# Last cross-attention of a decoder: values moved ahead of the fourth score, the last half in two units of 256 queries, the next maxima begun inside a unit

## The chip, the cores and the metric

The kernel runs on one core of a Trainium2 chip. The metric is device time in microseconds (us) for one execution, the median of several. Engines are named as the profile names them: PE is TensorE (PEld its weight loads), DVE is VectorE, ACT is ScalarE, POOL is GpSimd, and SP issues most of the DMAs. [...]

## The reference

The reference is a decoder of four layers over 1024 tokens of width 128. Each layer has self-attention, cross-attention to a context of 6404 rows, and a feed-forward part, each with a layer norm before it and added to `x`. The change touches the cross-attention of the last layer, which has 16 heads of 8 columns:

```python
q = _split_heads(Q @ Wq.T + bq)          # 1024 queries
k = _split_heads(K @ Wk.T + bk)          # 6404 keys
v = _split_heads(V @ Wv.T + bv)
scores = jnp.einsum('bhqd,bhkd->bhqk', q, k) / np.sqrt(D_HEAD)
scores = jnp.where(mask == 0, -1e9, scores)
attn = jax.nn.softmax(scores, axis=-1)
ctx = jnp.einsum('bhqk,bhkd->bhqd', attn, v)
return ctx.reshape(b, s, h * d) @ Wo.T + bo
```

The softmax needs the largest score of every query and head before the exponentials. The kernel therefore computes the scores twice: once with queries on the partitions, for the maxima, and once with keys on the partitions, for the exponentials and the values.

## The kernel before

Twelve stages follow each other, and the last cross-attention (`l3_xattn`, line 1650) is the last but one. Its operands are prepared earlier. Every number is split into three bf16 parts, so that one bf16 matmul over 64 partitions gives a product of nearly float precision for one head. `qPs[g]` and `kPs[g % 2]` hold queries and keys of group `g`: a group has four heads, as two pairs, and a pair is one tile of 128 partitions, one head in rows 0 to 63 and the other in rows 64 to 127. Keys of two groups fit in SBUF; `pairs_read` (line 1249) fetches those of groups 2 and 3 through SP's DMA queue once groups 0 and 1 are done.

The work is cut into eight **units**: four groups of heads by two halves of 512 queries. One unit is one call of `pairs_core` (line 1304). It walks over 51 key tiles (50 of 128 keys and one of 4). For each key tile it issues, for each of four heads, a score matmul (tile `s`, 128 keys by 512 queries) and an exponential on ScalarE (L1352, into `p`). After the fourth head's score it issues the four value matmuls of the *previous* key tile (`values`), which add onto `acc`: four heads in four column groups of the PE, 9 columns each, the ninth giving the sum of the softmax.

Beside each unit run the **maxima of the next one** (`pairs_max`, line 1258): a generator of 52 steps, 13 chunks of 512 keys by four tiles of 128 queries. One step has two parts, one per pair; each part issues two matmuls into a tile `m2` and one reduction on VectorE (L1280). `pairs_core` takes one step per key tile, between the second head's score and the third. There being 52 steps and 51 key tiles, the last step comes after the last values. When the steps are used up, the generator runs `pairs_neg` (line 1285): it reduces the maxima (L1290), splits them into three bf16 parts with small VectorE operations (L1293 to L1296), transposes them on the PE (L1300), and adds them to rows of `qP` kept free for that (L1302), so that the next unit's score matmuls subtract the maxima by themselves. `pairs_norm` (line 1368) then transposes the unit's result, divides it by its sum, and writes it to `o`.

[...]`ps = _Psum(ps0, m2=2, s=3, acc=1)`. That is two tiles `m2` of two banks each, three tiles `s`, and one `acc`. A fourth score has to wait until the exponential that reads the oldest of the three `s` tiles is done.

The framework's scheduler orders the instructions of each engine by their place in the program, but takes a later one first where an earlier one is not ready. `self.matmul` (line 261) marks a matmul that must keep the program's order among those so marked on the PE; scores, maxima and values in this loop are all marked, the transposes are not.

The first layer's self-attention (`l0_attn`, line 519) uses the same functions with a causal mask, and the third layer's cross-attention uses `pairs_core` with exponentials of double width.

Of the kernel before, what the change touches and what calls it, by code (L numbers as in the profile page):

```python
# [10 lines left out]
F32 = mybir.dt.float32  # L11
BF16 = mybir.dt.bfloat16
# [7 lines left out]
P = 128  # L20
# [194 lines left out]
class Decoder:  # L215
# [303 lines left out]
    def l0_attn(self):  # L519
# [6 lines left out]
        with tc.tile_pool(name="a", bufs=2) as pool:  # L526
# [39 lines left out]
            with tc.tile_pool(name="a1", bufs=2) as pool1, tc.tile_pool(name="a1_ps", bufs=2, space=PSUM) as ps0:  # L566
                ps = _Psum(ps0, m2=2, s=3, acc=1)

                def maxima(n):
                    if n < 8:  # L570
                        return self.pairs_max(ps, pool1, qPs[n % 4], kPs[n % 4], n // 4, mpad, S, causal)
                    return ()

                for step in maxima(0):
                    step(0)
                    step(1)
                for n in range(8):
                    g, h = n % 4, n // 4
                    oT = pool1.tile([P, BANK], F32, tag="oT", name="oT")
                    self.pairs_core(ps, pool1, qPs[g], kPs[g], v, g, h, oT, AF.Exp, 64, maxima(n + 1), causal=causal)  # L580
                    self.pairs_norm(ps, pool1, oT, o, g, h)
            with tc.tile_pool(name="a2", bufs=2) as pool2, tc.tile_pool(name="a2_ps", bufs=2, space=PSUM) as ps0:
                self.small_out(_Psum(ps0, m=8), pool2, o, wo)

# [670 lines left out]
                at = 16 * (2 * g + i)  # L1255
                self.nc.sync.dma_start(out=t[:, a:b], in_=src[at:at + 16, :, a:b].rearrange("p i c -> (p i) c"))

    def pairs_max(self, ps, pool, qP, kP, h, mpad, nk=NK, causal=None):

        nc = self.nc
        chunks = h + 1 if causal is not None else (nk + BANK - 1) // BANK
        mx = pool.tile([P, 4, 4, chunks], F32, tag="mx", name="mx")
        for c in range(chunks):
            for t in range(4):
                q0 = h * BANK + t * P
                a, b = c * BANK, min((c + 1) * BANK, nk if causal is None else q0 + P)

                def step(pair, a=a, b=b, q0=q0, t=t, c=c):
                    diag = causal is not None and b == q0 + P
                    m = ps.tile([P, 2, BANK], F32, tag="m2", name="m2")
                    for j in range(2):
                        r = slice(64 * j, 64 * j + 64)
                        self.matmul(m[:, j, :b - a], lhsT=qP[pair][r, q0:q0 + P], rhs=kP[pair][r, a:b], start=True, stop=not diag)
                    if diag:
                        for j in range(2):
                            self.matmul(m[:, j, b - a - P:b - a], lhsT=causal[:, 1, :], rhs=causal[:, 0, :], start=False, stop=True)
                    nc.vector.tensor_reduce(mx[:, t, 2 * pair:2 * pair + 2, c:c + 1], m[:, :, :b - a], AX.X, ALU.max)  # L1280

                yield step
        self.pairs_neg(ps, pool, qP, h, mpad, mx)

    def pairs_neg(self, ps, pool, qP, h, mpad, mx):

        nc = self.nc
        r = pool.tile([P, 4, 4], F32, tag="r", name="r")
        part = pool.tile([P, 4, 4], BF16, tag="part", name="part")
        nc.vector.tensor_reduce(r, mx, AX.X, ALU.max, negate=True)  # L1290
        mp = mpad.rearrange("p a t (j r) -> p t a j r", r=64)
        for i in range(3):
            nc.vector.tensor_copy(part, r)  # L1293
            nc.vector.tensor_copy(mp[:, :, :, :, 7 + 8 * i], part.rearrange("p t (a j) -> p t a j", a=2))
            if i < 2:
                nc.vector.tensor_tensor(r, r, part, ALU.subtract)  # L1296
        m = ps.tile([P, 2, BANK], F32, tag="m2", name="m2")
        for pair in range(2):
            for t in range(4):
                nc.tensor.transpose(m[:, pair, t * P:(t + 1) * P], mpad[:, pair, t, :], self.ident)  # L1300
            q = qP[pair][:, h * BANK:(h + 1) * BANK]
            nc.vector.tensor_tensor(q, q, m[:, pair, :], ALU.add)  # L1302

    def pairs_core(self, ps, pool, qP, kP, v, g, h, oT, func, rows, beside=None, between=None, causal=None):

        nc = self.nc  # L1310
        acc = ps.tile([P, BANK], F32, tag="acc", name="acc")
        nc.vector.memset(acc, 0.0)
        wide = beside is None
        matmul = nc.tensor.matmul if wide else self.matmul
        beside = iter(beside or ())
# [4 lines left out]

        def values(t, n, off, ws):
            for j in range(4):
                matmul(acc[32 * j:32 * j + v.shape[3], off:], lhsT=v[:n, t, 4 * g + j, :], rhs=ws[j][:n, :BANK - off],  # L1323
                       start=t == 0, stop=t == nkt - 1, tile_position=(0, 32 * j))

        for t in range(nkt):
            n = min(P, nk - t * P)
            off = 0 if causal is None else max(t * P - h * BANK, 0)
            w, hs = BANK - off, slice(h * BANK + off, (h + 1) * BANK)
            diag = causal is not None and t >= 4 * h  # L1330
            step = next(beside, None)
            ws = []
            for pair in range(2):
                both = None
                if wide:
                    both = ps.tile([P, 2, BANK], F32, tag="s", name="s")
                    p2 = pool.tile([P, 2, BANK], F32, tag="p", name="p", bufs=5)
                    ss, pp = [both[:, 0, :], both[:, 1, :]], [p2[:, 0, :], p2[:, 1, :]]
                else:
                    ss = [ps.tile([P, BANK], F32, tag="s", name="s") for _ in range(2)]  # L1340
                    pp = [pool.tile([P, BANK], F32, tag="p", name="p", bufs=10) for _ in range(2)]
                for j in range(2):
                    r = slice(64 * j, 64 * j + rows)
                    matmul(ss[j][:n, :w], lhsT=kP[pair][r, t * P:t * P + n], rhs=qP[pair][r, hs], start=True, stop=not diag)  # L1344
                if diag:
                    for j in range(2):
                        matmul(ss[j][:, :P], lhsT=causal[:, 0, :], rhs=causal[:, 1, :], start=False, stop=True)
                if wide:
                    nc.scalar.activation(p2[:n], both[:n], func)  # L1349
                else:  # L1350
                    for j in range(2):
                        nc.scalar.activation(pp[j][:n, :w], ss[j][:n, :w], func)  # L1352
                ws += pp
                if step and pair == 0:
                    step(0)
                    step(1)
            if late:
                values(*late.pop(0))
            late.append((t, n, off, ws))
            if between is not None:  # L1360
                next(between, None)
        values(*late.pop(0))
        for step in beside:
            step(0)
            step(1)
        self.copy(oT, acc)

    def pairs_norm(self, ps, pool, oT, o, g, h):

        nc = self.nc  # L1370
        m = ps.tile([P, 2, BANK], F32, tag="m2", name="m2")[:, 0, :]
        for i in range(4):
            nc.tensor.transpose(m[:, i * P:(i + 1) * P], oT[:, i * P:(i + 1) * P], self.ident)
        mv = m.rearrange("p (t j r) -> p t j r", t=4, r=32)
        rd = pool.tile([P, 4, 4], F32, tag="rd", name="rd")
        nc.vector.reciprocal(rd, mv[:, :, :, 8])
        ov = o[:, 4 * h:4 * h + 4, 32 * g:32 * g + 32].rearrange("p t (j r) -> p t j r", r=8)
        nc.vector.tensor_tensor(ov, mv[:, :, :, 0:8], rd[:, :, :, None].to_broadcast([P, 4, 4, 8]), ALU.mult)

    def l2_xattn(self):  # L1380
        nc, tc = self.nc, self.tc
# [268 lines left out]
    def l3_xattn(self):  # L1650
# [5 lines left out]
        with tc.tile_pool(name="x", bufs=2) as pool:  # L1656
# [27 lines left out]
                    next(vs, None)  # L1684
            with tc.tile_pool(name="x1", bufs=2) as pool1, tc.tile_pool(name="x1_ps", bufs=2, space=PSUM) as ps0:
                ps = _Psum(ps0, m2=2, s=3, acc=1)

                def maxima(n):
                    if n < 8:
                        return self.pairs_max(ps, pool1, qPs[n // 2], kPs[n // 2 % 2], n % 2, mpad)  # L1690
                    return ()

                for n in range(8):
                    g, h = n // 2, n % 2
                    oT = pool1.tile([P, BANK], F32, tag="oT", name="oT")
                    self.pairs_core(ps, pool1, qPs[g], kPs[g % 2], v, g, h, oT, AF.Exp, 64, maxima(n + 1))
                    if h == 1 and g < 2:
                        self.pairs_read(kPs[g], kd, g + 2, NK)
                    self.pairs_norm(ps, pool1, oT, o, g, h)
            with tc.tile_pool(name="x2", bufs=2) as pool2, tc.tile_pool(name="x2_ps", bufs=2, space=PSUM) as ps0:  # L1700

                nc.vector.tensor_tensor(o, o, bv[:, None, :].to_broadcast([P, NT, D]), ALU.add)
# [94 lines left out]
```

## Time and profile before

| | |
|---|---|
| median of 3 runs | 6444.39 us (6440.16 to 6455.54) |
| profiled execution | 6445.11 us, span 6443.3 us, mean granted PE clock 0.942 |
| PE busy | 5978.2 us, 93% of the span |
| DVE busy | 3473.1 us, 54% |
| ACT busy | 2999.3 us, 47% |
| loop of the last cross-attention | from about 5229 us to 6250 us of the span |
| maxima reductions (L1280), whole kernel | 928 instructions, 1026.8 us |
| exponentials (L1352), whole kernel | 1824 instructions, 924.7 us |

The page's busy times cover the whole kernel, and most of them belong to stages that the change leaves alone. [...] The useful views are the chain of work that ended last, the timeline inside one unit, the groups of instructions with different shapes kept apart, and the table of stretches, which also gives the PE clock that was granted. In the timeline a row gives the start, the time from the first start to the last end of the instructions merged in it, the engine, line and shapes, and in brackets the idle time before and what ended it.

### The profile page before, as it was taken

Reading aid. Unit: us, or ns where it says so; the run is one execution under the profiler, and the core shown is the slowest. Engines: PE = TensorE matmul, PEld = TensorE weight load, DVE = VectorE, ACT = ScalarE, POOL = GpSimd, SP = SyncE. Lnnn points to the kernel's source line nnn. Section 1 sums busy time; section 2 is a strip of 40 time slices with the busy share of each in tenths; the row PEclk is TensorE's granted clock in tenths of the full one; section 3 lists DMA queues with packets and bytes.
Section 4 is the critical chain, followed back from the end, with each engine's and each line's share of the span. In section 5 each row is a group of like instructions: output and inputs, shape, how many; then the busy total and the mean of one; then the engine's idle time right before and its main releaser. Section 6 shows DMA issues by size and latency. Waiting matters only on the chain. (4 is left out here: it accounts for less than half of the span.)

```text
span 6443.3 us, 78699 instructions
## 1 busy us (share of the span) xinstructions
PE 5978.2 (93%) x30428; PEld 2195.2 (34%) x30428; DVE 3473.1 (54%) x6685; ACT 2999.3 (47%) x4049; POOL 2231.0 (35%) x1074
## 2 busy tenths in 40 slices
PE   6799999999999999999899968999988779999979
PEld 2233333434343434343475433111134211111126
DVE  5476666666666666664224152100024799999913
ACT  2323333343433333334211226999921048788872
POOL 1026766677776767678331530100001000000000
PEclk7699999999999999999989978999999779999999
DMA  3000000000000000000000013200002100000000
GB/s 101 4 1 1 1 1 1 1 1 1 1 1 1 1 1 1 1 6 7 32 5 10 1 61 93 69 16 1 1 7 77 52 1 21 1 21 1 1 6 28
DMA packets 60845, 102.46 MB, mean 16 GB/s; under 512 B 10014, under 2 KB 46134, under 8 KB 58422
## 3 DMA queue, kind: packets, MB, share of 16 engines
q1 hardware_dynamic: 59894, 94.16, 4.7%
q8 instruction: 238, 3.90, 0.3%
q10 hardware_dynamic: 576, 3.28, 0.2%
q14 instruction: 137, 1.12, 0.1%
HBM read 66.01 MB, written 31.34 MB: 15 GB/s over the span
## 5 line engine op out<-in xcount | busy, mean ns | idle before, releaser
L755 POOL TENSOR_TENSOR tot<-tot,p 128x1024 f32<-128x1024 f32 (+1 forms) x800 | 1886.1, 2358 | 669.2 <-ACT p L747 636.0
L674 DVE CUSTOM_DVE_ANT_0 junk<-m,bars 128x512 f32<-128x512 f32 (+1 forms) x1664 | 1112.8, 669 | 620.3 <-PE m L671 492.3
L747 ACT ACTIVATE p<-s,drop,keep 128x1024 f32<-128x1024 f32 (+1 forms) x416 | 501.1, 1205 | 1487.4 <-PE s L740 1473.8
L1280 DVE TENSOR_REDUCE mx<-m 128x2 f32<-128x1024 f32 (+4 forms) x928 | 1026.8, 1155 | 89.0 <-PE m L263 78.6
L1352 ACT ACTIVATE p<-s 128x512 f32<-128x512 f32 (+3 forms) x1824 | 924.7, 590 | 272.9 <-PE s L263 272.2
L671 PE MATMUL m<-kT,qT 64*128 64x512 f32 (+1 forms) x3328 | 942.0, 608 | 1.1 <-DVE mx L674 0.8
L735 PE MATMUL s<-qT,kT 64*128 64x512 f32 (+1 forms) x3264 | 832.9, 599 | 9.6 <-DVE p L745 9.6
L722 PE MATMUL acc<-p,v 128*64 128x512 f32 (+1 forms) x3264 | 791.2, 605 | 0.8 <-ACT p L747 0.8
L1349 ACT ACTIVATE p<-s 128x1024 f32<-128x1024 f32 (+1 forms) x816 | 751.1, 1172 | 23.9 <-PE s L1344 23.9
L745 DVE TENSOR_TENSOR p<-s,every 128x1024 f32<-128x1024 f32 x400 | 489.7, 1224 | 198.3 <-PE s L735 111.5
L1323 PE MATMUL acc<-p,v 128*8 128x512 f32 (+1 forms) x3264 | 552.1, 596 | 0.0
L747 ACT ACTIVATE p<-p,drop,keep 128x1024 f32<-128x1024 f32 x400 | 492.8, 1232 | 44.3 <-DVE p L745 44.1
L263 PE MATMUL m<-kP,qP 64*128 64x512 bf16 (+4 forms) x1856 | 372.7, 397 | 116.9 <-DVE mx L1280 57.1
L263 PE MATMUL acc<-p,v 128*9 128x512 f32 (+3 forms) x3648 | 476.6, 595 | 0.0
L671 PEld LDWEIGHTS m<-kT,qT 64*128 64x128 f32 x3328 | 306.2, 186 | 474.9 <-DVE mx L674 226.6
L735 PEld LDWEIGHTS s<-qT,kT 64*128 64x128 f32 (+1 forms) x3264 | 332.2, 187 | 396.1 <-issue 341.6
L263 PE MATMUL s<-qP,kP 64*128 64x512 bf16 (+3 forms) x1824 | 435.4, 387 | 31.6 <-ACT p L1352 28.8
L722 PEld LDWEIGHTS acc<-p,v 128*64 128x64 f32 (+1 forms) x3264 | 197.0, 136 | 530.3 <-issue 527.4
L269 DVE COPY oT<-acc 128x512 f32<-128x512 f32 x16 | 11.0, 688 | 536.9 <-PE acc L1323 301.3
L1344 PE MATMUL s<-qP,kP 48*128 48x512 bf16 (+1 forms) x1632 | 249.2, 383 | 1.6 <-ACT p L1349 1.6
L263 PEld LDWEIGHTS <-qP 64*128 64x128 bf16 x1856 | 122.7, 96 | 335.2 <-issue 265.9
L263 PEld LDWEIGHTS <-kP 64*128 64x128 bf16 x1824 | 93.9, 94 | 402.0 <-issue 394.7
(446 smaller groups left out, 4995.6 us busy)
## 6 DMA issues: line engine op xcount, KB each, us to landing
kd<-part SPq DMA_DIRECT2D x156, 128.0 KB
kP<-kd SPq DMA_DIRECT2D x24, 512.0 KB
kP<-kd SPq DMA_DIRECT2D x48, 192.0 KB
w_expert<-in_Y_w SPq DMA_DIRECT2D x8, 768.0 KB
qd<-part SPq DMA_DIRECT2D x36, 128.0 KB
qP<-qd SPq DMA_DIRECT2D x16, 256.0 KB
w_decay<-in_c_decay SPq DMA_DIRECT2D x4, 1024.0 KB
ctxT<-in_ctxT ACTq DMA_DIRECT2D x4, 800.5 KB
```

The source lines that it names most:

```text
L263: return self.tc.keep_in_program_order(self.nc.tensor.matmul(*a, **k))
L671: nc.tensor.matmul(m[:, :b - a], lhsT=qT[r, q0:q0 + P], rhs=kT[r, a:b], start=True, stop=True)
L674: nc.vector.tensor_tensor_reduce(junk[:, :b - a], m[:, :b - a], bars[:, a:b], 1.0, -3.0e38, ALU.add, ALU.max, mx[:, t, j, c:c + 1])
L722: nc.tensor.matmul(acc[64 * j:64 * j + 64, :], lhsT=v[:n, t, 64 * j:64 * j + 64], rhs=pr[:n, j, :], start=t == 0, stop=t == NKT - 1, tile_ ...
L735: nc.tensor.matmul(s[:n, j, :], lhsT=kT[r, t * P:t * P + n], rhs=qT[r, hs], start=True, stop=t > t0)
L745: nc.vector.tensor_tensor(pr[:n], s[:n], every[:n], ALU.add)
L747: nc.scalar.activation(pr[:n], s[:n], AF.Exp, bias=drop[:n, t:t + 1], scale=keep[:n, t:t + 1])
L755: nc.gpsimd.tensor_tensor(tot[:n], tot[:n], pr[:n], ALU.add)
L1280: nc.vector.tensor_reduce(mx[:, t, 2 * pair:2 * pair + 2, c:c + 1], m[:, :, :b - a], AX.X, ALU.max)
L1323: matmul(acc[32 * j:32 * j + v.shape[3], off:], lhsT=v[:n, t, 4 * g + j, :], rhs=ws[j][:n, :BANK - off], start=t == 0, stop=t == nkt - 1, ...
L1349: nc.scalar.activation(p2[:n], both[:n], func)
L1352: nc.scalar.activation(pp[j][:n, :w], ss[j][:n, :w], func)
```

## The change

It has three parts, all in effect only in the last cross-attention.

1. In `pairs_core`, with maxima beside and no causal mask, the values of the previous key tile are issued before the fourth head's score instead of after it.
2. The last unit (group 3, second half) becomes two units of 256 queries, so there are nine units. The functions take a first query and a number of queries. From the seventh unit on, a step of the maxima is taken at every second key tile (`stride=2`); the maxima of a unit of 256 queries have 26 steps.
3. `pairs_neg` gets a function `after`. Between the small VectorE operations and the transposes it starts the maxima of the unit after the next and issues their first two steps. The transposes then use `s` tiles instead of an `m2` tile and keep the program's order on the PE. The next unit so begins with 50 steps left (24 for 256 queries), and the generator ends, with all of `pairs_neg`, at the top of the 51st key tile (index 50; index 48 where every second tile takes a step). Only in the first unit, which starts with 52 steps, does it still come after the last values.

```diff
@@ pairs_max
+        first = h * BANK if q0 is None else q0
-        mx = pool.tile([P, 4, 4, chunks], F32, tag="mx", name="mx")
+        mx = pool.tile([P, nq // P, 4, chunks], F32, tag=f"mx{nq}", name="mx", bufs=2 if nq == BANK else 1)
...
-            for t in range(4):
-                q0 = h * BANK + t * P
+            for t in range(nq // P):
+                q0 = first + t * P
...
-        self.pairs_neg(ps, pool, qP, h, mpad, mx)
+        self.pairs_neg(ps, pool, qP, first, nq, mpad, mx, after)
@@ pairs_neg
+        if after is not None:
+            after()
+        single = after is not None
+        m = None if single else ps.tile([P, 2, BANK], F32, tag="m2", name="m2")
+        transpose = (lambda *a: self.tc.keep_in_program_order(nc.tensor.transpose(*a))) if single else nc.tensor.transpose
         for pair in range(2):
-            for t in range(4):
-                nc.tensor.transpose(m[:, pair, t * P:(t + 1) * P], mpad[:, pair, t, :], self.ident)
-            q = qP[pair][:, h * BANK:(h + 1) * BANK]
-            nc.vector.tensor_tensor(q, q, m[:, pair, :], ALU.add)
+            mt = ps.tile([P, BANK], F32, tag="s", name="s") if single else m[:, pair, :]
+            for t in range(nt):
+                transpose(mt[:, t * P:(t + 1) * P], mpad[:, pair, t, :], self.ident)
+            q = qP[pair][:, first:first + nq]
+            nc.vector.tensor_tensor(q, q, mt[:, :nq], ALU.add)
@@ pairs_core
-            step = next(beside, None)
+            step = next(beside, None) if t % stride == 0 else None
...
                 for j in range(2):
+                    if not wide and causal is None and pair and j and late:
+                        values(*late.pop(0))
                     r = slice(64 * j, 64 * j + rows)
                     matmul(ss[j][:n, :w], lhsT=kP[pair][r, t * P:t * P + n], rhs=qP[pair][r, hs], start=True, stop=not diag)
...
-        self.copy(oT, acc)
+        self.copy(oT[:, :nq], acc[:, :nq])
@@ l3_xattn
+                units = [(g, h * BANK, BANK) for g in range(4) for h in range(2)]
+                units[-1:] = [(3, BANK, 256), (3, BANK + 256, 256)]
+                ready = []

                 def maxima(n):
-                    if n < 8:
-                        return self.pairs_max(ps, pool1, qPs[n // 2], kPs[n // 2 % 2], n % 2, mpad)
-                    return ()
+                    if n == len(units):
+                        return iter(())
+                    g, q0, nq = units[n]
+
+                    def after():
+                        steps = maxima(n + 1)
+                        for _ in range(2):
+                            step = next(steps, None)
+                            if step:
+                                step(0)
+                                step(1)
+                        ready.append(steps)
+
+                    return self.pairs_max(ps, pool1, qPs[g], kPs[g % 2], 0, mpad, q0=q0, nq=nq, after=after)
-                for n in range(8):
-                    g, h = n // 2, n % 2
+                steps = maxima(1)
+                for n, (g, q0, nq) in enumerate(units):
                     oT = pool1.tile([P, BANK], F32, tag="oT", name="oT")
-                    self.pairs_core(ps, pool1, qPs[g], kPs[g % 2], v, g, h, oT, AF.Exp, 64, maxima(n + 1))
-                    if h == 1 and g < 2:
+                    self.pairs_core(ps, pool1, qPs[g], kPs[g % 2], v, g, 0, oT, AF.Exp, 64, steps, q0=q0, nq=nq,
+                                    stride=1 if n < 6 else 2)
+                    if n in (1, 3):
                         self.pairs_read(kPs[g], kd, g + 2, NK)
-                    self.pairs_norm(ps, pool1, oT, o, g, h)
+                    self.pairs_norm(ps, pool1, oT, o, g, q0, nq)
+                    steps = ready.pop() if ready else iter(())
```

`pairs_norm` and the rest of these functions change only in that they take the first query and the number of queries.

## The prediction, before the result was known

> **What bounds the kernel now.** First the profiled execution's own numbers: span 6443.3 us, 6445.11 us in all, beside a median of 6444.39 us. The 1.8 us around the span and the 0.7 us between it and the median are left as they are; my sum is added to 6445.1. Only the last cross-attention changes (its loop lies at about 5229 to 6250 us), so I read the chain of waits there first. Columns: start, length, engine, tile, line.
>
> ```profile
> 5743.22 112.84 DVE mx L1280 x96
> 5861.52 2.08 PE acc L263 x16
> 5863.86 1.31 DVE mx L1280 x2
> 5871.50 112.84 DVE mx L1280 x96
> ...
> 6128.27 3.04 PE s L263 x6
> 6131.32 1.82 PE acc L263 x8
> 6247.67 2.10 PE acc L263 x16
> ```
>
> Each unit (512 queries, 51 key tiles) looks like 113 us of VectorE maxima. But the last unit, which has no maxima, also takes about 120 us. So I read the timeline: one key tile with maxima, then one of the last unit.
>
> ```profile
> 5423.00 0.39 PE L263 MATMUL s<-qP,kP 64*128 64x512 bf16 x2
> 5423.23 0.87 PE L263 MATMUL m<-kP,qP 64*128 64x512 bf16 x4
> 5423.43 2.06 ACT L1352 ACTIVATE p<-s 128x512 f32<-128x512 f32 x4 [0.29 <-PE s L263]
> 5423.92 0.53 PE L263 MATMUL s<-qP,kP 64*128 64x512 bf16 x2
> 5424.38 1.05 PE L263 MATMUL acc<-p,v 128*9 128x512 f32 x8
> 5425.36 0.39 PE L263 MATMUL s<-qP,kP 64*128 64x512 bf16 x2
> ...
> 6136.07 2.06 ACT L1352 ACTIVATE p<-s 128x512 f32<-128x512 f32 x4 [0.29 <-PE s L263]
> 6136.71 0.37 PE L263 MATMUL s<-qP,kP 64*128 64x512 bf16 x1 [0.47 <-ACT p L1352]
> 6137.02 1.04 PE L263 MATMUL acc<-p,v 128*9 128x512 f32 x8
> 6137.99 0.60 PE L263 MATMUL s<-qP,kP 64*128 64x512 bf16 x3
> 6138.42 2.07 ACT L1352 ACTIVATE p<-s 128x512 f32<-128x512 f32 x4 [0.29 <-PE s L263]
> ```
>
> Both repeat every 2.35 us, and in both ScalarE stands idle 0.29 us per tile, waiting for scores. VectorE is not the limit: in the pass before the loop, where nothing else runs, its reductions start 1.13 us apart (the matmuls before them start at 5109.86, 5110.99, 5112.12), 2.26 us a tile. ScalarE alone would need four starts of (2.06-0.59)/3 = 0.49: 1.96 us. The limit is a loop through the three "s" buffers. The fourth score waits until the first exponential has freed its buffer: 6136.71-6136.07 = 0.64. Values start 0.31 later and occupy the PE for 0.97. The next tile's first score then starts, and its exponential follows 0.43 later. 0.64+0.31+0.97+0.43 = 2.35.
>
> **Values ahead of the fourth score.** With three buffers, score k waits for exponential k-3, whatever stands between. Before: exponential 0, score 3, values, next score 0, its exponential. After: exponential 3, next tile's score 2, values, score 3, its exponential. Again four scores on, with the same four terms: 2.35 us. The PE's visible 0.47 wait is filled, and the wait reappears at the third score; ScalarE's 0.29 moves from the first exponential to the fourth. Maxima now stand between the second score (which waits for exponential 2) and the third: counted from one third score, the second score of the next tile comes at about 1.47, the two pairs at 1.5 and 1.97 (the latter held by the reduction before it), the third at 2.2, needed at 2.35. It just fits. Bounds: -0.09 a tile (down to VectorE's 2.26) to +0.05; I take +0.01 over 6x51 = 306 tiles: **+3 us** (ends -28, +15).
>
> **Two units of 256.** Removed: the last unit's 51 x 2.353 = 120 us. Added: 102 tiles of half width. No such loop is in the trace, but its terms are.
>
> ```profile
> L1352 ACT ACTIVATE p<-s 128x256 f32<-128x256 f32 x32 | 10.5, 381 | 15.1 <-PE s L263 15.1
> ...
> 163.97 0.83 PE L263 MATMUL acc<-p,v 128*9 128x384 f32 x8
> 164.74 0.23 PE L263 MATMUL s<-qP,kP 64*128 64x128 bf16 x2
> ```
>
> The exponential takes 0.38 instead of 0.59, so the first term is 0.43. A score streams 0.21 us at 512 columns and half at 256, so 0.31 becomes 0.20 and 0.43 becomes 0.32. Values occupy 0.97 at 512 columns and 164.74-163.97 = 0.77 at 384; on that line 256 takes 0.55 to 0.57, and I take 0.55. Sum 1.50; 102 x 1.50 = 153: **+33 us**. [...] The rows have fixed parts (0.38 against 0.59, and the handovers), and the path runs through them, so I use the rows. Ends: 114 (four ScalarE starts of 0.66-0.38 = 0.28) and 163.
> Halving the maxima beside the unit before (every second tile) gains nothing, since maxima did not set its 2.35.
>
> **The ends of the units.** Between starts at 5357.89 and 6000.19 lie five units: 128.46 each, 8.5 over 51 tiles. Today, after the last values, the last maxima step, the chain of small VectorE operations (5608.66 to 5610.38, 1.72), transposes and two additions follow each other with ScalarE idle. After, from the second unit on, this stands ahead of the 51st tile. The program's order holds TensorE to: two steps of the following maxima, eight transposes (about 0.27 each), then the tile's scores. Only two "m2" buffers exist, so the third and fourth pair of maxima wait for reductions, and behind them on the PE wait the transposes, four scores, the values of tile 49; ScalarE waits for those scores. From the third score of tile 49: reductions end near 0.9, chain 2.8, two reductions 5.1, transposes 5.4 to 7.6. The additions stand behind two more reductions in VectorE's queue (8.0 and 8.7) and free the two "s" buffers that the transposes took, so the third score is at 8.8 instead of 2.35: 6.45 late. At the unit's end, values of tile 50 wait for their own exponentials and the new unit has no values in its first tile: 1.25. Together 7.7. If the maxima are queued between the pieces of the chain, it is 9.3:
>
> ```profile
> 5608.27 0.48 DVE L1312 MEMSET acc<- 128x512 f32 x1
> 5608.66 0.31 DVE L1290 TENSOR_REDUCE r<-mx 128x16 f32<-128x208 f32 x1
> ```
>
> Here a memset written much later in the program went ahead of the chain, so ready work does slip in; I lean to 9.3. Memset and normalisation (0.48+0.26+0.29) now meet running maxima: up to +1. Against 8.5 that is -0.8 to +1.8; I take +1.5 for five units: **+7.5**. The first unit begins with 52 steps left, so its chain still follows its values, with two steps (up to 4.5 us of reductions) now inside it: **+4** (2 to 5). Seventh unit's end: fewer transposes, about -1. The extra end, without further maxima: chain 1.85, transposes 1.1, wait of the last values 0.9, about +4; half-width final copy and transposes -1. Together **+2**.
> Key reads on SP stay behind the second and fourth unit; their first reader comes some 6 us earlier, over 100 us after the issue: nothing. The first attention layer keeps its order: nothing.
>
> **Sum:** 3+33+7.5+4+2 = +49.5: 6445.1+49.5 is about **6495 us**.
>
> **Rivals.**
> *The half-width units run at half clock.* [...] The trace shows both outcomes; columns after the stretch are busy times of PE, weight loads, VectorE, ScalarE and GpSimd, then the granted clock.
>
> ```profile
> 230.00:235.00 5.00, 4.74 (x22) 0.39 (x20) 0.00 (x0) 3.43 (x7) 0.00 (x0) 0.50 0.00 0
> ...
> 6136.00:6140.00 4.00, 3.06 (x24) 0.44 (x20) 0.00 (x0) 3.65 (x8) 0.00 (x0) 1.00 0.00 0
> ```
>
> A unit without maxima entered at 0.50 stayed there 30 us at "4.74 of 5"; the present last unit, entered at 0.50 too, rose within 6 us and held 1.00 at 77% busy. A half-width tile at 0.50 takes 0.43+0.31+0.99+0.43 = 2.16, +0.66: 34 us a unit, 6529 with one, 6563 with both. [...]and I take 1.00. Chance 0.12.
> *Filling the wait does free the loop* (the faster side). Were the fourth score's wait the cost, and not the buffer count, units 1 to 6 would fall to VectorE's 2.26 (306 x 0.093 = -28), the seventh to ScalarE's 1.96 (-20), the halves to 102 x 1.12 = 114 (-6), with the ends +13.5: about -41, 6404. It decides once a 512-wide tile drops below about 2.20 us on average. For it: 0.47 of PE idle. Against it: ScalarE waits for the PE in every tile. Chance 0.10.
> *The ends almost vanish* (the change as good as does nothing in all). If PE and ScalarE lost 4 instead of 8.5 us at six ends, -27, beside +36: about 6454. Against it: two reductions and eight transposes stand ahead of the scores, 4.4 us by themselves. Chance 0.09.
>
> **How the numbers follow.** My case has 0.69, its own range 6470 to 6525. Below 6460 lie the faster case and most of the neutral one (0.16), above 6545 the fully cold one (0.04): 6460 to 6545 holds 0.8. 0.3% is 19 us, about what a measurement here tells from no change. Faster 0.10, same 0.09, slower 0.81.
>
> **What would show it.** In the new timeline: exponential starts in 512-wide tiles still 2.35 apart, with ScalarE's idle before the fourth; half-width tiles 1.5 apart at clock 1.00; a hole of 6 to 8 us in ScalarE before the 51st tile; a loop 45 to 55 us longer. Wrong if 512-wide tiles fall to 2.2, half-width ones to 1.2, or the hole before tile 51 is under 3 us.

## The result and the profile after

The changed kernel takes 6557.28 us (median of four runs, 6552.55 to 6559.3); the kernel before, on the same day, 6449.97 us. The ratio is 1.0165, with a 95% interval of 1.0149 to 1.0182: about 107 us slower. The direction was forecast, the size was not: 49.5 us were, and the range ended at 6545. All four runs have a mean granted clock of 0.930 or 0.931; the profiled one of the kernel before has 0.942. The differences given below with the three parts alone are taken from the ratios; the medians give 3 to 6 us more.

The profiled execution has a span of 6557.5 us against 6443.3. To see where the time lies, I use the starts of the copies of a finished unit (`oT<-acc`), one per unit, in the timelines of the two kernels. Each row is the time from one copy to the next. In the kernel before it holds the end of one unit and the tiles of the next; in the changed kernel the small operations of an end stand ahead of the copy, and only the first unit's stand behind it, so the second row holds two ends.

| interval ending with | before, us | after, us | difference |
|---|---|---|---|
| first unit (from ScalarE's table load) | 122.6 | 125.0 | +2.4 |
| second unit | 128.3 | 143.7 | +15.4 |
| third to sixth unit, sum | 513.6 | 545.0 | +31.4 |
| seventh unit | 128.7 | 134.6 | +5.9 |
| last half | 129.2 | 82.1 + 110.6 | +63.4 |

Together +118.5 us; work ahead of this loop happened to be some 6 us quicker in that execution.

The chain of waits of the changed kernel, one unit's end (start, length, engine, tile, line):

```profile
5872.87 2.37 DVE mx L1282 x2
5884.46 1.23 DVE mx L1282
5889.63 1.94 PE s L1304 x8
5893.34 1.82 PE acc L263 x8
5895.67 2.62 PE acc L263 x8
```

A maximum, the transposes (L1304) and then two sets of values stand in a row, and the values take 1.82 us and more where 1.05 was usual. The timeline inside a unit, after:

```profile
5421.74 2.06 ACT L1365 ACTIVATE p<-s 128x512 f32<-128x512 f32 x4 [0.29 <-PE s L263]
5422.44 0.37 PE L263 MATMUL s<-qP,kP 64*128 64x512 bf16 x1
5422.75 1.04 PE L263 MATMUL acc<-p,v 128*9 128x512 f32 x8
...
5424.15 2.06 ACT L1365 ACTIVATE p<-s 128x512 f32<-128x512 f32 x4 [0.34 <-PE s L263]
```

ScalarE still waits in every tile. The tiles are 2.41 and 2.35 us in turn, 2.38 on average: the moved values gained nothing and lost 0.03 us a tile. The end of the second unit, after:

```profile
5476.01 0.81 PE L263 MATMUL m<-kP,qP 64*128 64x512 bf16 x4
...
5477.93 0.39 PE L263 MATMUL m<-kP,qP 64*128 64x512 bf16 x2 [1.10 <-DVE mx L1282]
...
5479.13 0.39 PE L263 MATMUL m<-kP,qP 64*128 64x512 bf16 x2 [0.81 <-DVE mx L1282]
...
5481.82 1.94 PE L1304 MATMUL s<-ident,mpad 128*128 128x128 f32 x8 [2.29 <-DVE mpad L1297]
...
5484.31 1.06 ACT L1365 ACTIVATE p<-s 4x512 f32<-4x512 f32 x2 [7.28 <-PE s L263]
...
5485.45 1.89 PE L263 MATMUL acc<-p,v 128*9 128x512 f32 x8
...
5487.79 2.68 PE L263 MATMUL acc<-p,v 4*9 4x512 f32 x8
...
5490.51 0.69 DVE L269 COPY oT<-acc 128x512 f32<-128x512 f32 x1 [6.02 <-PE acc L263]
```

The PE waits 1.10, 0.81 and 2.29 us with little between, and ScalarE 7.28. After that, values take 1.89 us: the PE runs at half clock when it comes out (the granted clock is 0.50 from 5481 to 5494 us). An end of the kernel before has its wait behind the values, both sets of which take 2.15 us there:

```profile
5604.44 2.15 PE L263 MATMUL acc<-p,v 128*9 128x512 f32 x16
...
5610.54 1.08 PE L1300 MATMUL m<-ident,mpad 128*128 128x128 f32 x4 [3.61 <-DVE mpad L1294]
...
5614.15 1.08 ACT L1352 ACTIVATE p<-s 128x512 f32<-128x512 f32 x2 [6.93 <-PE s L263]
```

The last unit, after; the table of stretches gives the busy times of PE, weight loads, VectorE, ScalarE and GpSimd, then the granted clock:

```profile
6248.00:6250.00 2.00, 1.36 (x15) 0.29 (x12) 0.00 (x0) 1.59 (x6) 0.00 (x0) 1.00 0.00 0
...
6251.00:6252.00 1.00, 1.00 (x9) 0.19 (x8) 0.00 (x0) 0.37 (x1) 0.00 (x0) 1.00 0.00 0
6252.00:6253.00 1.00, 0.48 (x3) 0.29 (x2) 0.70 (x2) 0.00 (x0) 0.00 (x0) 0.63 0.00 0
...
6280.00:6320.00 40.00, 35.08 (x228) 4.76 (x224) 0.00 (x0) 23.26 (x76) 0.00 (x0) 0.50 0.01 1
```

The clock fell at about 6252.3 us, just behind the last tile (four keys) of the unit before, and stayed at 0.50 to the end of the loop, 110 us later.

### The profile page after: what moved, and what is told of

The parts are those of the page before. It is cut to its first block, busy times and chain, and to the rows that moved or that the text cites. A ratio compares the mean times of both kernels' runs of the same rounds, so it can differ in the third digit from the quotient of the medians.

```text
span 6557.5 us, 80141 instructions
## 1 busy us (share of the span) xinstructions
PE 6083.3 (93%) x31026; PEld 2233.7 (34%) x31040; DVE 3476.5 (53%) x6699; ACT 3020.3 (46%) x4254; POOL 2230.0 (34%) x1074
## 5 line engine op out<-in xcount | busy, mean ns | idle before, releaser
L1365 ACT ACTIVATE p<-s 128x512 f32<-128x512 f32 (+2 forms) x2028 | 946.3, 548 | 355.5 <-PE s L263 354.6
L263 PE MATMUL m<-kP,qP 64*128 64x512 bf16 (+4 forms) x1856 | 435.9, 401 | 115.8 <-DVE mx L1282 69.3
L263 PE MATMUL s<-qP,kP 64*128 64x512 bf16 (+2 forms) x2028 | 493.0, 379 | 51.4 <-ACT p L1365 48.6
L263 PE MATMUL acc<-p,v 128*9 128x512 f32 (+2 forms) x4056 | 521.6, 583 | 0.0
L263 PEld LDWEIGHTS <-kP 64*128 64x128 bf16 (+1 forms) x2028 | 101.2, 95 | 434.2 <-issue 427.3
## 6 DMA issues: line engine op xcount, KB each, us to landing
kd<-part SPq DMA_DIRECT2D x156, 128.0 KB
qd<-part SPq DMA_DIRECT2D x36, 128.0 KB
```

Source lines behind the costliest of these rows:

```text
L263: return self.tc.keep_in_program_order(self.nc.tensor.matmul(*a, **k))
```

## The experiments

**Each part alone.** The parts come apart cleanly in the source. The first part alone keeps the moved values, and has the last half whole and the next maxima where they were:

```diff
-                units[-1:] = [(3, BANK, 256), (3, BANK + 256, 256)]
-                                    stride=1 if n < 6 else 2)
+                                    stride=1)
-                    return self.pairs_max(ps, pool1, qPs[g], kPs[g % 2], 0, mpad, q0=q0, nq=nq, after=after)
+                    return self.pairs_max(ps, pool1, qPs[g], kPs[g % 2], 0, mpad, q0=q0, nq=nq)
-                    steps = ready.pop() if ready else iter(())
+                    steps = maxima(n + 2) if n + 2 <= len(units) else iter(())
```

> Only the first part: values ahead of the fourth score; eight units, ends as before. Theory (three score buffers set 2.35 us a tile wherever the values stand; with maxima now between the second and the third score the tile reads 2.38 in the changed kernel's trace): 357 tiles x 0.03 = +8 to +11 us, about 6460; the last unit, without maxima, stays at 2.35 a tile. Rival (filling the PE's visible wait frees the loop and the loss lies elsewhere): tiles of 2.26 or less, -28 us or more, at most 6425.

6467.62 us, ratio 1.0024 (1.0015 to 1.0033): about +15 us. From copy to copy its units take 130.2 to 130.9 us instead of 128.3 to 128.7, 14.7 us over the first seven; that is the theory's direction at more than its size (8 to 11), and the rival is gone. Its last unit took 14 us more in the profile for another reason: it ran at 0.50 for its first 45 us, where the last unit of the kernel before had risen to 1.00 within 6. This profile is of the slowest of the kernel's twenty runs (6481.72 us, mean clock 0.937; the fastest 6455.72 and 0.943), so those 14 us look like that run's, not the kernel's.

The second part alone has neither `after=` nor the moved values, and keeps the two half-width units:

```diff
-                    if not wide and causal is None and pair and j and late:
-                        values(*late.pop(0))
...
-                    return self.pairs_max(ps, pool1, qPs[g], kPs[g % 2], 0, mpad, q0=q0, nq=nq, after=after)
+                    return self.pairs_max(ps, pool1, qPs[g], kPs[g % 2], 0, mpad, q0=q0, nq=nq)
...
-                    steps = ready.pop() if ready else iter(())
+                    steps = maxima(n + 2) if n + 2 <= len(units) else iter(())
```

> Only the second part: the last half as two units of 256 queries, values after the fourth score, ends as before. Theory: the unit of 256 with maxima beside takes 1.50 us a tile at full clock, the one without maxima 2.14 us at half clock: 76 + 109 - 120 = +65 and one more end of 5 to 8: +65 to +75 us, about 6520. Rival (the half clock of the last unit comes only with the other two parts): 76 + 76 - 120 + 8 = +40, about 6490.

6504.76 us, ratio 1.0077 (1.0056 to 1.0098): about +50 us, between the two expectations. The trace decides: the halves take 80.8 and 112.3 us against 129.2 (+64), and the last unit is at 0.50 from 6202 to 6310 us, its end. (The whole loop is 70 us longer in that trace, and the work ahead of it happened to be 9 us quicker.) So the half clock comes with the split, not with the other two parts. Here the PE was busy for 1.64 of the 4 us ahead of that unit (6198 to 6202).

The third part alone keeps `after=` and takes the other two out:

```diff
-                    if not wide and causal is None and pair and j and late:
-                        values(*late.pop(0))
-                units[-1:] = [(3, BANK, 256), (3, BANK + 256, 256)]
-                                    stride=1 if n < 6 else 2)
+                                    stride=1)
```

> Only the third part: next maxima begun ahead of the transposes, in eight units of 512 queries, values after the fourth score. Theory: the ends of the units cost 13 us instead of 8.5 whatever the order of the values: +4.5 to +6 us at seven ends, +32 to +42, about 6487. Rival (the ends grew because the values stand ahead of the fourth score): under +10 us, about 6458.

6473.96 us, ratio 1.0033 (1.0024 to 1.0042): about +21 us, under the theory's numbers and over the rival's. Unit by unit: the second interval grew by 14 us (the first unit's late end lies in it), the next four by 4 to 6, and the last two shrank by about 3. The theory had the size of an ordinary end right and multiplied it by too many ends. (This profile, too, is of the slowest of twenty runs.)

**The last unit's clock.** Two kernels add matmuls beside the last unit, whose results nothing reads; where the dots stand are two matmuls into `m`, as in `pairs_max`, without a reduction.

```diff
+                def filler(n, k):
+                    g, q0, nq = units[n]
+                    for c in range(k):
+                        def step(pair, c=c):
+                            m = ps.tile([P, 2, BANK], F32, tag="m2", name="m2")
...
+                        yield step
-                    steps = ready.pop() if ready else iter(())
+                    steps = (filler(8, 26) if n == 7 else ready.pop()) if ready else iter(())
```

> The changed kernel with maxima matmuls beside the last unit too, at every second tile as in the unit before; nothing reads their results. Theory (256-wide tiles without maxima keep the PE too idle for full clock): the last unit holds 1.00 at 1.50 us a tile, -30 to -33 us, about 6526. Rival (tiles of the last unit are slow for another reason than the clock): 0 or more, 6557 or above.

6524.41 us, ratio 1.011 (1.0089 to 1.0132). The last unit fell from 110.6 to 80.6 us by *added* work, with the clock at 1.00 from 6260 to 6320 us: the clock is the cause of those 30 us. The second kernel fills only 16 tiles (`filler(8, 16)`, at every tile).

> The changed kernel with maxima matmuls beside the first 16 tiles of the last unit only, at every tile; nothing reads their results. Theory (the density of the PE's work in each tile sets the clock): 1.00 while they last, back to 0.50 within some 10 us after tile 16 and to the end: 16 to 20 tiles x 0.64 = -10 to -13 us, about 6545. Rival (one idle gap at the change of units threw the clock, and warmth once gained is kept): 1.00 to the end, -30 us, about 6527.

6523.5 us, ratio 1.0115 (1.0084 to 1.0145): here my theory fell. The stretches of this kernel:

```profile
6240.00:6245.00 5.00, 3.63 (x35) 1.20 (x32) 2.50 (x12) 3.12 (x11) 0.00 (x0) 1.00 0.01 3
6245.00:6250.00 5.00, 4.83 (x30) 0.73 (x29) 0.00 (x0) 2.38 (x8) 0.00 (x0) 0.50 0.00 0
...
6252.00:6254.00 2.00, 1.68 (x12) 0.81 (x11) 0.00 (x0) 1.59 (x6) 0.00 (x0) 0.50 0.00 0
...
6256.00:6258.00 2.00, 2.00 (x24) 0.65 (x24) 0.00 (x0) 1.71 (x7) 0.00 (x0) 1.00 0.00 0
...
6280.00:6300.00 20.00, 15.13 (x161) 3.98 (x164) 0.00 (x0) 16.25 (x55) 0.00 (x0) 1.00 0.00 1
```

The filler ends at about 6275 us, and the same tiles that had stayed at 0.50 for 109 us now stay at 1.00 for 50 us, with the PE busy 76% of the time. So these tiles went on at 1.00 behind the filler and at 0.50 without it. (Without added matmuls they were at 0.50 in two more profiles: from 6202 to 6310 us with the second part alone, from 6250 to 6320 us with the late normalisation below. The half before took 87.1 us here instead of 82.1.)

The first two stretches also show where the clock fell in this kernel: at 6245.0 us, ahead of the four-key tile of that unit, whose values come 3.7 us later:

```profile
6248.71 1.55 PE L263 MATMUL acc<-p,v 4*9 4x256 f32 x8
```

So the four-key tile is not needed for the fall.

**The end of a unit.** First, the normalisation written later:

```diff
+            if then is not None and t == 1:
+                then()
...
-                    self.pairs_norm(ps, pool1, oT, o, g, q0, nq)
+                    then = lambda oT=oT, g=g, q0=q0, nq=nq: self.pairs_norm(ps, pool1, oT, o, g, q0, nq)
```

> The changed kernel with each unit's normalisation (transposes of its result, division) written after the second tile of the next unit. Theory (at a unit's end the next scores stand on the PE behind those transposes, which wait for the copy of the result: 1.7 us at the ends seen): -1.5 to -3 us at eight ends, -12 to -20, about 6541. Rival (the half clock after the stall is all of the extra end): within 4 us of 6557.

6553.0 us, ratio 1.0161 (1.0136 to 1.0186), not to be told from the changed kernel, as the rival said; that the half clock is *all* of the extra end, as it also said, this run does not show. The next scores do start ahead of the copy then, but third to sixth unit still take 136.2 to 136.5 us. Then the kernel before, with its chain of small operations brought forward and no following maxima in front of the transposes:

```diff
             step = next(beside, None)
+            more = next(beside, None) if step and causal is None and t in (48, 49) else None
...
+                if more and pair == 0:
+                    more(0)
+                    more(1)
```

> The kernel before, with one edit: tiles 48 and 49 of a unit take two maxima steps each (the short ones of 260 keys), so that the small VectorE operations and the transposes come at the 51st tile, without any step of the following maxima ahead of them. Theory (what costs in the third part is the two steps ahead of the transposes and the clock lost in that stall, not the earlier place): the ends fall from 8.5 to 3 to 6 us, -18 to -38 over seven ends, about 6422. Rival (transposes in front of a tile's scores cost as much as after the last values): within 8 us of 6450.

6471.02 us, ratio 1.0038 (1.0027 to 1.0049): 21 us slower by the medians, against both expectations. The units take 130 to 133 us. In its timeline the PE waits 0.3 to 0.7 us for reductions inside tiles 48 and 49, ScalarE stands 3.9 us before the 51st tile, and the last two sets of values follow at 0.50 (3.72 us for both). I read from this that a stall of the PE *ahead of values* is what costs, with or without maxima in it. To see what of that is clock, I held the clock in the third part's stall:

```diff
+        mts = [ps.tile([P, BANK], F32, tag="s", name="s") for _ in range(2)] if single else None
+        if single:
+            after(lambda k: [self.matmul(mts[0], lhsT=kP[0][:, 0:P], rhs=kP[0][:, P:P + BANK], start=True, stop=True) for _ in range(k)])
...
                                 step(0)
+                                busy(4 * i)
                                 step(1)
+                                busy((3, 9)[i])
```

> The third part alone, with sixteen matmuls per unit added in the stall (between the two steps of the following maxima, and between the last of them and the transposes); they write into a score tile that the transposes then overwrite, so nothing reads them. Theory (the half clock that the stall leaves behind, through two sets of values at 1.85 us instead of 0.97, makes much of the ends' growth): the clock stays at 1.00 through the stall, an end costs 2.5 to 3.5 us less, and the kernel 15 to 25 us less than the third part alone: about 6455. Rival (the place of the work in the queues is all of it): within 6 us of the third part alone, 6474.

6461.03 us, ratio 1.0017 (1.0007 to 1.0027), 13 us less than the third part alone by the medians and 10 by the ratios, whose intervals just overlap; 15 to 25 were expected. From copy to copy, third to sixth unit take 129.0 to 131.8 us instead of 132.7 to 134.2. The last two intervals are 2 and 3 us longer instead, and in this execution the last unit's tiles came 3.63 us apart from 6144.14 to 6158.65 us, then 2.35. Both sets of values at one unit's end, third part alone (clock 0.50 from 5634 to 5644 us):

```profile
5637.88 3.71 PE L263 MATMUL acc<-p,v 128*9 128x512 f32 x16
```

and with the clock held (1.00 from 5602 to 5616 us):

```profile
5613.82 2.24 PE L263 MATMUL acc<-p,v 128*9 128x512 f32 x16
```

**The buffer loop, and a version that beats both.** In the last unit no maxima run, so their two tiles lie idle:

```diff
+                    if spare and pair == 0:
+                        both = ps.tile([P, 2, BANK], F32, tag="m2", name="m2")
+                        ss = [both[:, 0, :], both[:, 1, :]]
+                    else:
                         ss = [ps.tile([P, BANK], F32, tag="s", name="s") for _ in range(2)]
...
-                    self.pairs_core(ps, pool1, qPs[g], kPs[g % 2], v, g, h, oT, AF.Exp, 64, maxima(n + 1))
+                    self.pairs_core(ps, pool1, qPs[g], kPs[g % 2], v, g, h, oT, AF.Exp, 64, maxima(n + 1), spare=n == 7)
```

> The kernel before, with one edit: in its last unit, which has no maxima, the first two heads' scores go to the two idle maxima tiles, so that seven banks hold scores instead of three. Theory (the three buffers set the 2.35 us): the last unit goes to ScalarE's pace of 1.96 to 2.0 us a tile, 51 x 0.36 = -18 us, about 6432. Rival (PE and ScalarE would need 2.35 us anyway): 0, 6450.

6427.15 us, ratio 0.9964 (0.9954 to 0.9974), about 23 us less: the last interval falls from 129.2 to 108.3 us. Its values, tile by tile:

```profile
6160.69 1.22 PE L263 MATMUL acc<-p,v 128*9 128x512 f32 x8
...
6162.65 1.21 PE L263 MATMUL acc<-p,v 128*9 128x512 f32 x8
```

1.96 us apart, ScalarE's own pace. With fifteen added matmuls at each end as well (they write into the tile that the transposes overwrite):

```diff
+        for _ in range(busy):
+            self.matmul(m[:, 1, :], lhsT=kP[0][:, 0:P], rhs=kP[0][:, P:P + BANK], start=True, stop=True)
```

> The kernel before, with the first two heads' scores of the last unit in the idle maxima tiles, and with fifteen added matmuls at each unit's end while the small VectorE operations run; they write into the tile that the transposes then overwrite, so nothing reads them. Theory (the ends of the kernel before, too, lose time to half clock after 3.6 us of idle PE): transposes take 0.63 instead of 1.08 us and the first tiles run at full clock, 1 to 2.5 us an end: 7 to 17 us less than with the spare tiles alone (6427), about 6415. Rival (the ends wait for VectorE, not for the PE): within 4 us of 6427.

6422.18 us, ratio 0.9949 (0.9934 to 0.9964), the fastest of all. The mean granted clock of the profiled execution is 0.945, against 0.942 with the spare tiles alone. At the end that follows 5604 us the first four transposes take 0.60 instead of 1.08 us; VectorE's wait for them is 1.09 us at each of the first five ends, and 1.27 at every end of the kernel before. Second to sixth unit take 127.3 to 127.7 instead of 128.0 to 128.7. That is 0.9 us an end, under the 1 to 2.5 expected; the seventh unit, ahead of which that wait was 2.77 us, took 129.4 instead of 128.8. The medians of the two differ by 5 us, between the theory's 7 and the rival's 4, and their intervals overlap.

**The whole change with its clock held**, both fillers together:

> The whole change, with added matmuls that nothing reads, in two places: sixteen per unit in the stall ahead of the transposes, and maxima matmuls beside the first 16 tiles of the last unit. Theory (the step of the forecast that failed is the clock; its other terms stand): about 34 us less for the last unit and 3 us less at each of seven ends, 6557 - 34 - 15 to 21 = 6502 to 6508, near the 6500 that the forecast's +49.5 gives on this day's 6450. Rival (another cost is left out of the forecast): over 6520.

6507.0 us, ratio 1.0099 (1.0075 to 1.0122), mean granted clock of the profiled execution 0.943 instead of 0.930. The time is the expected one, but the kernel before ran at 6441.36 beside it, so the difference is 64 us (48 to 79), not 57. The intervals of its trace sum to +68 against those of the kernel before: 50 of the 118.5 us went with the clock, 30 in the last unit and 21 in the ends, less rounding.

## Why the prediction was wrong

**What held.** *The buffer loop.* "Again four scores on, with the same four terms": the move freed nothing, and giving the loop more buffers did at once (2.35 to 1.96; tried only in the last unit, where no maxima run). The faster rival is excluded by the first part alone. *The half-width tile.* 1.50 us was forecast from four rows; in the trace the four exponentials of a tile begin at 6240.84, those of the next at 6242.34 and 6243.84. At half clock, 2.16 was forecast and 2.14 measured (values at 6257.45 and 6259.59). With the clock held the two halves cost +33.7 us, against "+33 us" and a part of the "+2".

**Where it failed: the clock.** The step is "and I take 1.00", an estimate of mine that none of the rows quoted shows for half-width tiles. The rival beside it had the price (34 us a unit, 0.12 of the chance) and came true for one of the two units. In the changed kernel no gap of the PE shown from 6244 to 6253 us is longer than 0.52 us, yet the clock fell at the change of units, and it stayed at 0.50 for 109 us with the PE shown 88% busy. A fall was to be expected: in the profile of the kernel before the clock is at 0.50 for 3 to 10 us behind every end (behind the seventh from 6124 to 6134 us). The question was whether it comes back to 1.00 in half-width tiles. And what I quoted for safety (a unit that rose within 6 us and then held 1.00 at 77% busy) was the outcome of one entry; the row above it, at 0.50 for 30 us, was the other. The same failure sits in "the ends of the units": every term there was priced at full clock, values at 0.97, although a stall ahead of values was just what the part made. "Together 7.7", or 9.3, became 14 to 16 us (135.4 to 137.2 less 51 tiles of 2.38); the fillers took about 21 us out of the seven ends, and about 3 out of an ordinary one in the third part alone.

**Smaller misses, by size.** *Values ahead of the fourth score:* "+3 us" was about +13 for six units, at the upper end of the bounds given (+15). I had the maxima "just fit" between the second and the third score with 0.15 us to spare; the trace shows every other tile late by 0.06. That their second pair waits for the reduction before it is my reading of the order, not shown by a run. *The ends at full clock:* 22 us or so instead of 13.5. From the kernel with the clock held: third to sixth unit take 132.1 to 133.2, of which 2.2 is the values' move, so +2.3 an end where +1.5 was taken; the second interval grew 12 us where its parts summed to about 8. The queue order that I leaned to (maxima between the pieces of the chain) is what the trace has: transposes came 7.1 us after the third score of tile 49, where 5.4 was written and the slower reckoning's 1.6 more make 7.0. The normalisation's transposes, which I had not placed ahead of the next scores, are there, but moving them gained nothing.

**Sum.** Forecast +49.5; with the clock held +64 (48 to 79) measured, +68 in the trace. Of the 18 or so between forecast and trace, 10 are the values' move and about 8 the ends. The rest, from 64 to 107 measured and from 68 to 118.5 in the traces, went with the clock.

**What stays open.** What makes the clock fall at the end of a half-width unit, where no gap of the PE shown in the changed kernel was longer than 0.52 us. The four-key tile is not needed (the kernel with 16 filled tiles fell at 6245.0 us, 3.7 us ahead of that tile's values); what else stands there, no run here separates. Nor does one show why a full-width unit without maxima came back to 1.00 after 6 us in one profile and after 45 us in another.

## What to carry to other kernels

Where a few PSUM buffers in rotation set the pace, as three did here, look for another buffer before moving work along the rotation: the move turned 2.35 us a tile into 2.38, two idle tiles turned it into 1.96. Before a stall is moved, look at what runs behind it: behind the moved stall two sets of values took 3.71 us, and 2.24 with the clock held. Useless matmuls can pay: some twenty microseconds of them at the entry of the last unit brought this kernel from 6557.28 to 6523.5 us. And a profile is one execution: before a unit's time is put down to a change, see in which clock it ran.

## What the runs showed of the hardware that was not expected

The same half-width tiles ran 109 us at 0.50 (PE busy 88% by the profile) in the changed kernel, and 50 us at 1.00 (busy 76%) behind some 20 us of added matmuls at their start. The fall came without a long idle: the largest gap of the PE shown around it, from 6244 to 6253 us, was 0.52 us. A unit of full width without maxima was at 0.50 for its first 6 us in the profile of the kernel before, and for 45 in that of the first part alone (the PE busy 37.40 of the 40 us from 6150 to 6190, at 0.50), which alone is 14 us of a result. Runs of one kernel spread as well: the twenty of the first part alone span 26 us, and on the whole the slower ones have the lower mean clock (0.937 in the slowest, 0.943 in the fastest).
